# Cross-attention with LayerNorm: another order of the odd slot's work on TensorE, ScalarE and VectorE

## The chip, the core and the metric

The kernel runs on one core of a Trainium2 chip. A core has a matrix engine (TensorE, PE in the profile; its weight loads are PEld), a vector engine (VectorE, DVE), an engine for activation functions (ScalarE, ACT), a general engine (GpSimd, POOL) and SyncE (SP), which here only issues transfers. Each engine works through its own queue in order; semaphores make an instruction wait for one on another engine. The metric is the device time of one execution, in microseconds (us).

## The reference

Four batches of 2048 rows of x (512 wide) attend, in 16 heads of 32, to 77 rows of a context; then output projection, residual and LayerNorm:

```python
qs = (q @ wq).reshape(Bq, Lq, H, HD).transpose(0, 2, 1, 3)
ks_ = (k @ wk)...;  vs = (v @ wv)...
scores = jnp.einsum('bhqd,bhkd->bhqk', qs, ks_) / jnp.sqrt(jnp.float32(HD))
scores = jnp.where(mask[:, None, :, :], -jnp.inf, scores)
attn_w = jax.nn.softmax(scores, axis=-1)
attn = jnp.einsum('bhqk,bhkd->bhqd', attn_w, vs)
out = attn.transpose(0, 2, 1, 3).reshape(Bq, Lq, H * HD) @ wo + q
mu = jnp.mean(out, axis=-1, keepdims=True)
var = jnp.mean((out - mu) ** 2, axis=-1, keepdims=True)
return (out - mu) / jnp.sqrt(var + EPS) * gamma + beta
```

q is x, k and v are the context. All is float32.

## The kernel before

The 8192 rows are 64 tiles of 128 rows. Two tiles are a block, four a group; 16 tiles are a batch. Keys and values of all batches are made once at the start and stay on the chip. Each float32 matmul of a projection is three matmuls: operands are split into a high and a low part (hi*hi, hi*lo, lo*hi), so a projection of a tile is 12 matmuls of 128x128 by 512.

The stages of a tile t, with their engine and line:

- `load_xT`, `cast_xT` (ScalarE, L149), `split_xT` (GpSimd, L153): the transposed input, split in two parts; `q_visit` (TensorE, L160) and `q_evac` (VectorE, L177): queries, a quarter of a group in each slot.
- `scores` (TensorE, L284): 64 small matmuls of 32 rows into four banks of PSUM.
- `maxima` (VectorE, L298): for each of 16 heads, masked scores and their row maximum, each followed by a read of the accumulator.
- `exps` (ScalarE, L312): for each head, the exponential in place, with the row sum.
- `recip` (VectorE, L323) and `normalise` (GpSimd, L328): the reciprocal of the sums and one multiplication for all heads.
- `transp` (VectorE, L352) and `regroup` (12 transfers a block, issued by SP, L364): the weights transposed and laid out for the next product.
- `av` (TensorE, L382): the values' product of a block, 32 matmuls of 96x32 by 256; `av_hi` (ScalarE, L413) and `av_lo` (VectorE, L417): its result split into AH and AL.
- `o_proj` (TensorE, L446), `residual` (VectorE, L455), `moments` (VectorE L460 and L465, then four small operations on GpSimd, L469 to L472, in the odd tile).
- `scale` (ScalarE, L478), `affine` (GpSimd, L482 gamma and L483 beta), `store` (SP, L486).

A loop runs over 27 even tiles u (n = u/2 is the block). One turn has an even slot for tile u and an odd slot for tile u + 1. The stages overlap over several blocks: while tile u has its scores taken, the values' product belongs to block n - 2, the output projections to tiles u - 6 and u - 5, the scales to u - 8 and u - 7. The last ten tiles follow an order written out by hand (`ORDER`), which the change does not touch.

The order of the calls in the program is the order of each engine's queue; there is no scheduler. Three further things set the order of the work. All results of TensorE go through eight PSUM banks that are handed out in a ring, so a new tile waits until the tile eight allocations earlier is read out. `pbuf` (scores, exponentials and weights of a tile) has three buffers. AH and AL have two each, one block per buffer.

Twice per batch VectorE also prepares the mask of the next batch in the even slot: `mask_bias` (L264, L265) in the turn of the batch's tile 12, `mask_nan` (L269 to L271) in that of tile 14; this happens in the first three batches.

The order in the even slot is, on ScalarE: `cast_xT`, 12 exponentials of u, two scales, the last 4 exponentials of u. In the odd slot it is, on TensorE: scores, values' product, output projection, queries; on ScalarE: 4 exponentials of u + 1, the two casts of AH, 12 exponentials; on VectorE: 12 maxima of u + 1, reciprocal of u, 4 maxima, first AL, residual, second AL, transposition of u, moments, reciprocal of u + 1.

Of the kernel before, what the change touches and what calls it, by code (L numbers as in the profile page):

```python
# [19 lines left out]
H = 16  # L20
# [47 lines left out]
def xattn_layernorm(  # L68
# [26 lines left out]
    def bank(name):  # L95
        return ps.tile([P, 512], F32, tag="mm", name=name)
# [37 lines left out]
    def keys_of(h):  # L134
        return slice(TAIL_K, NK2) if h % 2 == 0 else slice(0, NK)
# [6 lines left out]
    def load_xT(g, c):  # L142
        fx[g, c] = sb.tile([P, 2, GRP], F32, tag="xtf", name=f"xtf_{g}_{c}")
        nc.sync.dma_start(fx[g, c], xT[g, :, c : c + 2])
# [29 lines left out]
    def q_evac(g, m):  # L174
        pq = qp.pop((g, m))
        if g:
            nc.vector.tensor_copy(qd[g][:, m, :], pq)  # L177
        else:
            nc.vector.tensor_copy(qd[0][:, m : m + 2, BLK:], pq.rearrange("p (m r) -> p m r", m=2))
# [45 lines left out]
    def values_evac(b):  # L225
        pv = vd.pop(b)[:NK2].rearrange("p (q a d) -> p q a d", a=2, d=HD)
        for a in range(2):
            nc.vector.tensor_scalar(  # L228
                vsb[:, b].rearrange("p (q a d) -> p q a d", a=2, d=HD)[:, :, a], pv[:, :, a], vm[:, a, 0:1], None, ALU.mult
            )  # L230
# [43 lines left out]
    def scores(t):  # L274
        qs = qd[t // 4]
        nmax[t] = sb.tile([P, H], F32, tag="nm", bufs=3, name=f"nm_{t}")
        sums[t] = sb.tile([P, H], F32, tag="sum", bufs=3, name=f"sum_{t}")
        sc = scs[t] = [bank(f"sc_{t}_{j}") for j in range(GH)]
        for g in range(NG):
            for half in range(0, P, P // 2):  # L280
                for j in range(GH):
                    q = slice(HD * j, HD * (j + 1))
                    r0 = (t % 4) * P + half
                    nc.tensor.matmul(  # L284
                        sc[j][half : half + P // 2, g * NK : (g + 1) * NK],
                        qs[q, g, r0 : r0 + P // 2],
                        kct[q, g, t // TPB, keys_of(j)],
                        start=True,
                        stop=True,
                    )  # L290

    def maxima(t, lo, hi):
        pb = pbuf[t % NPB]
        mb = bat[t // TPB][0]
        nm = nmax[t]
        for h in HEADS[lo:hi]:
            g, j = divmod(h, GH)
            nc.vector.tensor_tensor_reduce(  # L298
                pb[:, h // 2, (h % 2) * NK : (h % 2 + 1) * NK],
                scs[t][j][:, g * NK : (g + 1) * NK],  # L300
                mb[:, t % TPB, keys_of(h)],
                -1.0,
                3.0e38,
                ALU.add,
                ALU.min,
                accum_out=nm[:, h : h + 1],
            )

    def exps(t, lo, hi):
        pb = pbuf[t % NPB]  # L310
        for h in HEADS[lo:hi]:
            nc.scalar.activation(  # L312
                pb[:, h // 2, (h % 2) * NK : (h % 2 + 1) * NK],
                pb[:, h // 2, (h % 2) * NK : (h % 2 + 1) * NK],
                AF.Exp,
                bias=nmax[t][:, h : h + 1],
                scale=-1.0,
                accum_out=sums[t][:, h : h + 1],
            )

    def recip(t):
        ris[t] = sb.tile([P, H], F32, tag="ri", bufs=3, name=f"ri_{t}")
        nc.vector.reciprocal(ris[t], sums[t])  # L323

    def normalise(t):
        pv = pbuf[t % NPB][:, :, : 2 * NK].rearrange("p q (a k) -> p q a k", a=2)
        rv = ris[t].rearrange("p (q a) -> p q a", a=2)[:, :, :, None]
        nc.gpsimd.tensor_tensor(pv, pv, rv.to_broadcast((P, NP, 2, NK)), ALU.mult)  # L328
# [15 lines left out]
    def transp(t):  # L344
        b, tt = divmod(t, 2)
        if b not in bts:
            bts[b] = sb.tile([P, 5, 2 * NP * 32], F32, tag="B", name=f"B_{b}")
        if b < NBLK - 1:
            bt = bts[b].rearrange("p c (q t r) -> p c q t r", q=NP, t=2)[:, :, :, tt, :]
        else:  # L350
            bt = bts[b].rearrange("p c (t q r) -> p c q t r", q=NP, t=2)[:, :, :, tt, :]
        nc.vector.transpose(  # L352
            bt.rearrange("p c q r -> p q c r"),
            pbuf[t % NPB].rearrange("p q (c r) -> p q c r", c=5),
        )
# [81 lines left out]
    def o_proj(t):  # L437
        b, tt = divmod(t, 2)
        rs = slice(tt * P, tt * P + P)
        ah, al = at[b]  # L440
        first = t not in pos
        if first:
            pos[t] = bank(f"po_{t}")
        for c in range(NC_D):
            for n, (a, w) in enumerate(((ah, woh), (ah, wol), (al, woh))):
                nc.tensor.matmul(  # L446
                    pos[t],
                    a[:, c, rs],
                    w[:, c, :],
                    start=(first and c == 0 and n == 0),  # L450
                    stop=(c == NC_D - 1 and n == 2),
                )

    def residual(t):
        nc.vector.tensor_tensor(od[t], pos.pop(t), od[t], ALU.add)  # L455
# [124 lines left out]
    def pieces(u):  # L580
        return casts.get(u) or [((u + 8) // 4, u % 4)] * (u + 8 < 4 * NGRP)

    evac = [(0, 0)]
    for u in range(0, 2 * CUT, 2):
        n = u // 2
        m, k = divmod(u, TPB)

        for q in pieces(u + 2):
            if u >= 4:
                load_xT(*q)  # L590
        for t in (u - 4, u - 3):
            if t >= 0:
                load_x(t)
        scores(u)
        maxima(u, 0, H // 2)
        for q in evac:
            q_evac(*q)
        maxima(u, H // 2, H)
        for q in pieces(u):
            cast_xT(*q)  # L600
        exps(u, 0, 3 * H // 4)
        for v in list(vd):
            values_evac(v)
        for q in pieces(u):
            split_xT(*q)
        if u == 0:
            mask_bias(0, slice(1, TPB))
            split_wv()
        if u >= 6:
            o_proj(u - 6)  # L610
        for v in {2: (0,), 4: (2, 3)}.get(u, ()):
            values(v)
        for q in visits(u):
            q_visit(*q)
        if u >= 6:
            residual(u - 6)
            moments(u - 6)
        if u == 4:
            transp(2)
        if u:  # L620
            transp(u - 1)
            regroup(n - 1)
        if u >= 8:
            scale(u - 8)
            scale(u - 7)
        exps(u, 3 * H // 4, H)
        if u >= 8:
            affine(u - 8)
        for q in visits(u):
            q_evac(*q)  # L630
        if u == 0:
            load_wo()
            nc.gpsimd.memset(ident, 0.0)
            nc.gpsimd.affine_select(ident, ident, [[-1, P]], ALU.not_equal, 1.0, base=0, channel_multiplier=1)
        if u == 2:
            split_wo(0)
            split_wo(1)
        if k == TPB - 6 and m + 1 < NB:
            load_mask(m + 1)
        if k == TPB - 4 and m + 1 < NB:  # L640
            mask_bias(m + 1)
        if k == TPB - 2 and m + 1 < NB:
            mask_nan(m + 1)

        scores(u + 1)
        maxima(u + 1, 0, 3 * H // 4)
        recip(u)
        maxima(u + 1, 3 * H // 4, H)
        exps(u + 1, 0, H // 4)
        normalise(u)  # L650
        if u >= 8:
            affine(u - 7)
        for v in list(vd):
            values_evac(v)
        if u >= 4:
            av(n - 2)
            av_hi(n - 2, 0)
            av_hi(n - 2, 1)
        exps(u + 1, H // 4, H)
        if u >= 5:  # L660
            o_proj(u - 5)
        if u >= 4:
            av_lo(n - 2, 0)
        if u >= 5:
            residual(u - 5)
        if u >= 4:
            av_lo(n - 2, 1)
        if u != 2:
            transp(u)
        for v in {2: (1,)}.get(u, ()):  # L670
            values(v)
        evac = visits(u + 1)
        for q in evac:
            q_visit(*q)
        if u == 2:
            load_xT(*pieces(4)[0])
        if u >= 5:
            moments(u - 5)
        if u == 0:
            mask_nan(0)  # L680
        if u == 2:
            split_wo(2)
            split_wo(3)
        recip(u + 1)
        normalise(u + 1)
        if u >= 8:
            store(u - 8)
            store(u - 7)
# [87 lines left out]
```

## Time and profile before

| what | value |
|---|---|
| median of 3 runs | 534.55 us (533.18 to 534.91) |
| the profiled execution | 533.62 us |
| its span, first to last instruction | 531.8 us |
| granted TensorE clock, mean | 0.996 |
| TensorE busy | 514.6 us, 97% |
| VectorE busy | 485.3 us, 91% |
| ScalarE busy | 459.4 us, 86% |
| GpSimd busy | 401.1 us, 75% |

The span falls into a start (to about 81 us, where tile 8 begins), 23 even turns of the loop (to 431 us) and the tail. A row of the timeline gives start, duration, engine, line, operation, the tiles written and read with their shapes, and in brackets how long the engine stood idle before and what released it. Matmuls overlap in the rows, so what a group of them takes is read from its start to the start of the next group. The chain of waits is followed back from the last instruction, so it names at each moment what the end depended on.

### The profile page before, as it was taken

The numbers are of one execution on the slowest core, as the hardware profiler recorded it, in microseconds if no ns is written. First come the engines' busy times: TensorE is split into PE (matmuls) and PEld (weight loads), VectorE is DVE, ScalarE is ACT, GpSimd is POOL, SyncE is SP. The second block draws the span as 40 slices with busy tenths as digits, with TensorE's granted clock in tenths as the row PEclk, the third lists the DMA queues.
The fourth block names the chain that finished last, engine by engine and source line by source line (L and its number), as shares of the span: only waits on it lengthen the run. The fifth ranks groups of instructions, "written<-read, shape, count | busy, mean of one in ns | idle before, by whom it ended". The sixth has DMA issues, their size and how long they took to land.

```text
span 531.8 us, 20432 instructions
## 1 busy us (share of the span) xinstructions
PE 514.6 (97%) x6858; PEld 393.0 (74%) x6858; DVE 485.3 (91%) x2592; ACT 459.4 (86%) x2215; POOL 401.1 (75%) x363
## 2 busy tenths in 40 slices
PE   8999999999999999999999999999999999998994
PEld 6977677777777777777777777777777777775672
DVE  5689889999999899889998998889999989999897
ACT  5687799998899999998899999998899999998500
POOL 0626537998799988887899888888799988665751
PEclk9999999999999999999999999999999999999998
DMA  8934757888778788887778788779777865859844
GB/s 303 403 119 110 216 148 183 234 210 221 212 185 219 216 226 211 217 208 206 200 201 226 206 222 220 190 188 254 188 201 215 229 187 160 220 141 272 230 135 158
DMA packets 58712, 110.24 MB, mean 207 GB/s; under 512 B 9392, under 2 KB 11056, under 8 KB 58608
## 3 DMA queue, kind: packets, MB, share of 16 engines
q1 hardware_dynamic: 55424, 102.64, 70.2%
q0 software_dynamic: 2304, 5.24, 3.5%
q10 hardware_dynamic: 880, 1.05, 0.8%
q8 instruction: 55, 0.90, 0.7%
q14 instruction: 49, 0.40, 0.2%
HBM read 41.79 MB, written 16.78 MB: 110 GB/s over the span
## 4 chain that ended last, share of the span: by engine, by line
PE 29%; ACT 28%; DVE 26%; DMA 9%; issue 3%; SPq 3%; POOL 1%; DVEq 0%; ACTq 0%
ACT pbuf L312 23%; PE po L446 10%; PE pq L160 9%; DVE pbuf L298 7%; DVE B L352 5%; DMA PT<-B 4%; PE pa L382 3%; PE sc L284 3%; DVE q L177 3%; DMA o<-x 3%; ACT AH L413 3%; SPq L364 2%; DVE st L460 2%; ACT o L478 2%; PE pk L186 1%
## 5 line engine op out<-in xcount | busy, mean ns | idle before, releaser
L312 ACT ACTIVATE pbuf<-pbuf,nm 128x77 f32<-128x77 f32 x1024 | 353.2, 356 | 30.0 <-DVE nm L298 24.8
L312 ACT ACTIVATION_READ_ACCUMULATOR pbuf<-pbuf,nm 128x1 f32 x1024 | 201.4, 197 | 0.0
L328 POOL TENSOR_TENSOR pbuf<-pbuf,ri 128x1232 f32<-128x1232 f32 x63 | 142.9, 2270 | 58.2 <-DVE ri L323 44.5
L298 DVE CUSTOM_DVE_ANT_0 pbuf<-sc,mb 128x77 f32<-128x77 f32 x1024 | 168.8, 230 | 3.1 <-PE sc L284 3.1
L446 PE MATMUL po<-woh,AH 128*128 128x512 f32 x256 | 108.6, 424 | 0.0
L446 PE MATMUL po<-wol,AH 128*128 128x512 f32 x256 | 100.2, 391 | 0.0
L446 PE MATMUL po<-woh,AL 128*128 128x512 f32 x256 | 100.1, 391 | 0.0
L160 PE MATMUL pq<-xth,wqh 128*128 128x512 f32 (+1 forms) x256 | 98.5, 385 | 0.1
L160 PE MATMUL pq<-xtl,wqh 128*128 128x512 f32 (+1 forms) x256 | 97.9, 382 | 0.0
L160 PE MATMUL pq<-xth,wql 128*128 128x512 f32 (+1 forms) x256 | 97.9, 382 | 0.0
L352 DVE STREAM_TRANSPOSE B<-pbuf 128x1280 f32<-128x1280 f32 x64 | 95.5, 1493 | 2.5 <-POOL pbuf L328 1.8
L298 DVE DVE_READ_ACCUMULATOR2_ANT nm<- 128x1 f32 x1024 | 84.3, 82 | 0.0
L284 PEld LDWEIGHTS sc<-kct,q 32*64 32x64 f32 x4096 | 51.9, 130 | 23.6 <-issue 16.5
L153 POOL TENSOR_TENSOR xtl<-xtf,xth 128x1024 fp32r<-128x1024 f32 x28 | 67.1, 2398 | 2.8 <-ACT xth L149 2.8
L382 PE MATMUL pa<-PT,vsb 96*32 96x256 f32 x992 | 60.2, 381 | 7.5 <-DMA o<-x 1.9
L483 POOL TENSOR_TENSOR o<-o,bet 128x512 f32<-128x512 f32 x48 | 63.2, 1316 | 3.8
L446 PEld LDWEIGHTS po<-woh,AH 128*128 128x128 f32 x256 | 48.0, 187 | 23.2 <-DVE nm L298 6.2
L284 PE MATMUL sc<-kct,q 32*64 32x77 f32 x4096 | 62.5, 238 | 0.4 <-DVE vsb L228 0.4
L482 POOL TENSOR_TENSOR o<-o,gam 128x512 f32<-128x512 f32 x48 | 61.8, 1287 | 0.6 <-ACT o L478 0.3
L446 PEld LDWEIGHTS po<-woh,AL 128*128 128x128 f32 x256 | 48.1, 188 | 10.9 <-DVE AL L417 0.3
L160 PEld LDWEIGHTS pq<-xth,wqh 128*128 128x128 f32 x256 | 48.1, 188 | 10.5 <-PE pq L160 0.5
L446 PEld LDWEIGHTS po<-wol,AH 128*128 128x128 f32 x256 | 48.2, 188 | 9.5 <-issue 1.4
(106 smaller groups left out, 670.9 us busy)
## 6 DMA issues: line engine op xcount, KB each, us to landing
PT<-B SPq DMA_DIRECT2D x346, 128.0 KB
xtf<-xT SPq DMA_DIRECT2D x28, 512.0 KB
o<-x SPq DMA_DIRECT2D x56, 256.0 KB
out<-o SPq DMA_DIRECT2D x56, 256.0 KB
PT<-B POOLq DMA_DIRECT2D x21, 128.0 KB, 5.1
o_end<-x SPq DMA_DIRECT2D x8, 256.0 KB
out<-o_end SPq DMA_DIRECT2D x8, 256.0 KB
xtf<-xT SPq DMA_DIRECT2D x4, 256.0 KB
```

The costliest lines, as they stand in the source:

```text
L153: nc.gpsimd.tensor_tensor(l, fx.pop((g, c)), h.bitcast(F32), ALU.subtract)
L160: nc.tensor.matmul(pq, w[:, c, m * P : (m + 1) * P], r[:, c, rs], start=(n == 0), stop=(n == 11))
L177: nc.vector.tensor_copy(qd[g][:, m, :], pq)
L284: nc.tensor.matmul(sc[j][half : half + P // 2, g * NK : (g + 1) * NK], qs[q, g, r0 : r0 + P // 2], kct[q, g, t // TPB, keys_of(j)], start= ...
L298: nc.vector.tensor_tensor_reduce(pb[:, h // 2, (h % 2) * NK : (h % 2 + 1) * NK], scs[t][j][:, g * NK : (g + 1) * NK], mb[:, t % TPB, keys_ ...
L312: nc.scalar.activation(pb[:, h // 2, (h % 2) * NK : (h % 2 + 1) * NK], pb[:, h // 2, (h % 2) * NK : (h % 2 + 1) * NK], AF.Exp, bias=nmax[t ...
L328: nc.gpsimd.tensor_tensor(pv, pv, rv.to_broadcast((P, NP, 2, NK)), ALU.mult)
L352: nc.vector.transpose(bt.rearrange("p c q r -> p q c r"), pbuf[t % NPB].rearrange("p q (c r) -> p q c r", c=5),)
L382: nc.tensor.matmul(pas[b, g // 2][HD * j : HD * (j + 1), (g % 2) * BLK : (g % 2 + 1) * BLK], vsb[:, 2 * b // TPB, HD * h : HD * (h + 1)], ...
L446: nc.tensor.matmul(pos[t], a[:, c, rs], w[:, c, :], start=(first and c == 0 and n == 0), stop=(c == NC_D - 1 and n == 2),)
L482: nc.gpsimd.tensor_tensor(o, o, gam, ALU.mult)
L483: nc.gpsimd.tensor_tensor(o, o, bet, ALU.add)
```

## The change

In the even slot all 16 exponentials of u run ahead of the two scales. In the odd slot the reciprocal of u stands ahead of all 16 maxima of u + 1; 12 exponentials of u + 1 run before the casts of AH and 4 after them; the output projection and its residual come before the values' product; and the transposition of u comes before both AL on VectorE. GpSimd's and SP's queues keep their order, and no instruction is added or removed.

```diff
@@ even slot
         for q in pieces(u):
             cast_xT(*q)
-        exps(u, 0, 3 * H // 4)
+        exps(u, 0, H)
...
             scale(u - 8)
             scale(u - 7)
-        exps(u, 3 * H // 4, H)
         if u >= 8:
             affine(u - 8)
@@ odd slot
+        recip(u)
         scores(u + 1)
-        maxima(u + 1, 0, 3 * H // 4)
-        recip(u)
-        maxima(u + 1, 3 * H // 4, H)
-        exps(u + 1, 0, H // 4)
+        maxima(u + 1, 0, H)
         normalise(u)
+        exps(u + 1, 0, 3 * H // 4)
         if u >= 8:
             affine(u - 7)
         for v in list(vd):
             values_evac(v)
+        if u >= 5:
+            o_proj(u - 5)
+            residual(u - 5)
         if u >= 4:
             av(n - 2)
             av_hi(n - 2, 0)
             av_hi(n - 2, 1)
-        exps(u + 1, H // 4, H)
-        if u >= 5:
-            o_proj(u - 5)
+        exps(u + 1, 3 * H // 4, H)
+        if u != 2:
+            transp(u)
         if u >= 4:
             av_lo(n - 2, 0)
-        if u >= 5:
-            residual(u - 5)
-        if u >= 4:
             av_lo(n - 2, 1)
-        if u != 2:
-            transp(u)
```

## The prediction

> **What bounds the kernel now.** I read the page first, then one pair of tiles by the windows, then the chain of waits, then the timeline of each engine. In the page, TensorE is busy nearly all the time:
>
> ```profile
> PE 514.6 (97%) x6858; PEld 393.0 (74%) x6858; DVE 485.3 (91%) x2592; ACT 459.4 (86%) x2215; POOL 401.1 (75%) x363
> ```
>
> One pair of tiles of the steady part, from the start of its even scores to the next, as a window (length, then busy time of TensorE, its weight loads, VectorE, ScalarE, GpSimd; granted clock):
>
> ```profile
> 217.93:233.11 15.18, 15.00 (x209) 11.57 (x208) 13.43 (x79) 14.45 (x70) 13.19 (x11) 1.00 0.80 214
> ```
>
> TensorE has 0.18 us to spare in 15.18, ScalarE 0.73, VectorE and GpSimd near 2, at granted clock 1.00. The chain of waits in the same stretch runs on TensorE alone (start, duration, group):
>
> ```profile
> 218.00 0.88 PE sc L284 x52
> 218.88 2.92 PE po L446 x12
> 221.80 2.72 PE pq L160 x12
> 224.52 0.97 PE sc L284 x52
> 225.50 0.09 issue
> 225.59 1.93 PE pa L382 x32
> 227.52 2.94 PE po L446 x12
> 230.46 2.72 PE pq L160 x12
> ```
>
> The even slot (first three rows) takes 6.52 us, the odd one 8.66. ScalarE is the next bound. Its one stop per pair is ahead of the even tile's exponentials, for the maxima:
>
> ```profile
> 219.21 0.36 ACT L312 ACTIVATE pbuf<-pbuf,nm 128x77 f32<-128x77 f32 x1 [0.73 <-DVE nm L298]
> ```
>
> So ScalarE, when late, can win back about 0.8 us a pair. The question is whether that survives.
>
> **TensorE.** No instruction is added or removed; the order on GpSimd's and SP's queues is unchanged. In the odd slot the order becomes scores, output projection, values' product, queries. The tail of the kernel shows these neighbours already:
>
> ```profile
> 436.08 2.92 PE pq L160 x12
> 439.00 1.86 PE pa L382 x32
> 440.87 0.88 PE sc L284 x52
> 441.75 2.94 PE pq L160 x12
> ```
>
> A full-width group between scores and values' product takes 2.92, one between two tiled groups 2.94, the values' product 1.86, scores 0.88. The new odd slot is 0.88 + 2.92 + 1.86 + 2.94 = 8.60, a gain of 0.06 a pair; over the 23 pairs from tile 8 to tile 54, 1.4 us, if TensorE stays the bound. Bounds: 8.40 if the switch from projection to values' product cost nothing (2.72 in place of 2.92), 8.69 if the 0.09 of issue came back.
>
> The Trainium skill, page "TensorEngine Tiling (Array Packing)", Key Properties, says that changing the tiling mode drains TensorE. The change makes one more passage between full and tiled matmuls per pair; by that rule, with about 0.1 us per drain as an estimate from the 0.09 above, it would cost some 2 us over the pairs. The rows of the tail say that the dear switch is the present one, between two tiled forms (0.97 + 0.09 against 0.88), so the trace does not bear the loss out; neither decides the sum.
>
> **VectorE: a new ring of waits.** Three moves lengthen one path. The two scales of finished tiles (L478) stand behind 16 exponentials instead of 12; GpSimd's affine of the tile (L482, L483) waits for the first of them and stands ahead of normalise(u); and on VectorE transp(u), which waits for normalise(u), now stands ahead of both av_lo, of the moments, of recip(u+1), and so of the next even tile's maxima. These feed the next exponentials. That closes a ring, one turn per pair. Its pieces:
>
> ```profile
> 32.95 2.26 POOL L328 TENSOR_TENSOR pbuf<-pbuf,ri 128x1232 f32<-128x1232 f32 x1 [6.29 <-DVE ri L323]
> ...
> 215.32 0.69 DVE L455 TENSOR_TENSOR o<-po,o 128x512 f32<-128x512 f32 x1 [1.59 <-PE po L446]
> 215.93 0.68 DVE L417 TENSOR_TENSOR AL<-pa,AH 128x512 fp32r<-128x512 f32 x1
> 216.53 1.50 DVE L352 STREAM_TRANSPOSE B<-pbuf 128x1280 f32<-128x1280 f32 x1
> 217.95 0.65 DVE L460 BATCH_NORM_STATS2 st<-o 128x6 f32<-128x512 f32 x1
> 218.64 0.18 DVE L465 BATCH_NORM_AGGREGATE mv<-st 128x2 f32<-128x6 f32 x1
> 218.74 0.22 DVE L323 RECIPROCAL ri<-sum 128x16 f32<-128x16 f32 x1
> 218.87 0.24 DVE L298 CUSTOM_DVE_ANT_0 pbuf<-sc,mb 128x77 f32<-128x77 f32 x1
> ...
> 262.00 4.12 ACT pbuf L312 x24
> 285.37 0.82 ACT L478 ACTIVATE o<-o,rn 128x512 f32<-128x512 f32 x1
> 286.27 1.28 POOL L482 TENSOR_TENSOR o<-o,gam 128x512 f32<-128x512 f32 x1 [0.15 <-ACT o L478]
> 287.63 1.29 POOL L483 TENSOR_TENSOR o<-o,bet 128x512 f32<-128x512 f32 x1
> ```
>
> From the first exponential: 16 exponentials 5.50 (4.12 for 12 of them with their accumulator reads); scale to gam 0.90 (285.37 to 286.27, a row that waited); gam to bet 1.36; bet 1.29; normalise 2.26; transposition 1.42 (216.53 to 217.95); two av_lo at 0.60 (215.93 to 216.53); stats 0.69; aggregate 0.10; reciprocal 0.13; first maximum to first exponential 0.34 (218.87 to 219.21). Sum: 15.19. In the kernel before the same ring has 12 exponentials and no av_lo: 1.38 and 1.20 less, 12.6, which ScalarE's own 14.4 hides.
>
> So the ring equals TensorE's new 15.1 within its error. I bound it by 14.9 (if GpSimd, like VectorE in these rows, where 216.53 + 1.50 lies past 217.95, starts an operation some 0.08 before the last has ended, three times) and 15.5 (0.08, as between the scale's end and gam, at four more hand-offs). Taken: 15.19, the sum of the rows. Steadily it costs nothing; but lateness of ScalarE, which the kernel before wins back, is now never won back.
>
> **Where ScalarE becomes late.** Six pairs carry mask work for the next batch on VectorE, between the even tile's query copy and the odd tile's maxima: three times L264 and L265, three times L269 to L271.
>
> ```profile
> 240.78 1.30 DVE L264 TENSOR_SCALAR mb<-m 128x1232 bf16<-128x1232 uint8 x1
> 242.00 1.40 DVE L265 TENSOR_SCALAR mb<-m 128x304 bf16<-128x304 uint8 x1
> 243.65 0.36 ACT L312 ACTIVATE pbuf<-pbuf,nm 128x77 f32<-128x77 f32 x1 [2.17 <-DVE nm L298]
> 257.00 1.42 DVE L269 TENSOR_REDUCE nz<-m 128x16 f32<-128x1232 uint8 x1
> ...
> 259.24 0.23 DVE L298 CUSTOM_DVE_ANT_0 pbuf<-sc,mb 128x77 f32<-128x77 f32 x1
> ```
>
> The third row: ScalarE stood 2.17 us for the odd tile's maxima. The reciprocal, now ahead of them, adds 0.25: it waits for the sixteenth exponential, here long done, so nothing but its own time. Of 2.42, 0.73 is taken up by the stop quoted above: 1.7 late. The other mask pair has 2.24 of work (257.00 to 259.24) where the first has 2.54: 1.4 late. Three of each: 9.3 us, all of it kept.
>
> How much of it TensorE can ignore: the next output projection needs the first av_lo. In the new ring that ends 14.7 after the even scores begin (1.28 to the first exponential, 12.73 of the ring's pieces to the end of the transposition, 0.69); the third matmul of the next projection wants it at 15.1 + 0.88 + 0.5 (two matmuls of 2.92/12) = 16.5. That is 1.8 to spare, so TensorE follows ScalarE once the latter is 1.8 late, that is from the first mask pairs (tile 16) on.
>
> **The start.** Tiles below 8 have no scales to separate the exponentials of two tiles, so the reciprocal ahead of the maxima now stops ScalarE:
>
> ```profile
> 63.61 0.25 DVE L323 RECIPROCAL ri<-sum 128x16 f32<-128x16 f32 x1 [1.48 <-ACT pbuf L312]
> 64.86 1.05 ACT L413 CAST AH<-pa 128x512 fp32r<-128x512 f32 x2
> 66.11 0.50 PE L446 MATMUL po<-woh,AH 128*128 128x512 f32 x1
> 84.56 0.38 ACT L312 ACTIVATE pbuf<-pbuf,nm 128x77 f32<-128x77 f32 x1
> 432.61 0.36 ACT L312 ACTIVATE pbuf<-pbuf,nm 128x77 f32<-128x77 f32 x1 [0.61 <-DVE nm L298]
> ```
>
> Before, ScalarE went straight on while VectorE waited 1.48. After, it waits for reciprocal and first maximum: 0.6 in tiles 4 and 6 each, of which a later stop takes part; tile 8 starts 0.9 late. The cast AH (64.86) stands eight exponentials further back, 2.75 + 0.6 later, so the first output projection (66.11) comes about 3 later. TensorE loses there the lead it had; afterwards ScalarE decides.
>
> **What else moves, at no cost.** residual(u-5) ahead of the transposition: its projection ends earlier, so VectorE's wait of 1.6 us goes, and the wait for normalise(u) comes late in its place (in the ring). The casts AH behind 12 exponentials instead of 4: the values' product itself is 2.9 later, and ScalarE reaches them after it. The affines end later and with them two stores on SP; behind these stand loads whose data are wanted a pair later. The regrouping transfers follow transp(u-1), which does not move, and are wanted a pair later.
>
> **The sum.** ScalarE reaches tile 8 at 84.56 + 0.9 = 85.5 and tile 54 at 85.5 + 23 x 15.19 + 9.3 = 444.2. Before: 432.61. That is 11.6 late; TensorE, with its 1.8 to spare, is 9.8 late. I let the tail keep 9.8: the profiled 533.62 (span 531.8 and 1.8 around it) becomes 543.4. The runs' median is 0.93 above the profiled execution, so 544.
>
> **Rivals.**
> 1. *The lateness is won back.* If the ring is 14.8 or less, 0.3 a pair comes back; six pairs lie between mask pairs, and only 3.1 - 1.8 = 1.3 of each double reaches TensorE: 3 x 1.3 + 3 at the start - 1.4 gives +5.5, 540; without the start's share 537. For it: the overlaps of 0.08. Against: eleven pieces read from rows would have to be 0.4 too long together.
> 2. *Faster.* TensorE stays the bound and its odd slot falls to 8.40, the bound above: 0.26 x 23 = 6.0 won, less 3 of the start, 531.5. It decides only if the ring stays under 14.9; the rows of 2.92 and 2.94 speak against.
> 3. *A longer ring,* 15.5, hand-offs paid in full: 23 x 0.3 more, 551.
> 4. *Nothing happens:* gain and loss meet, 534.5; only the late start being hidden would allow it.
>
> **How the numbers follow.** Forecast (540 to 548) 0.55; rival 1 (537 to 540) 0.20; rival 3 0.10; rival 4 0.05; rival 2 0.10. A measurement of this kernel tells about 0.3%, 1.6 us. Slower: 0.85. The range 536.5 to 549 leaves out rivals 2 and 4 and the outer part of 3. With cases of one sign holding 0.85, no second range is needed.
>
> **What would show it.** Right: GpSimd's gam waits for the scale (ACT o L478) in nearly every pair; VectorE waits for normalise at its transposition; TensorE stops in the even output projection for AL in the mask pairs; pairs of 15.2 and six of 16.5 to 16.9; ScalarE's tile 8 at 85.5. Wrong: pairs below 15.0, ScalarE still stopping 0.7 for the maxima in each pair, or mask pairs followed by pairs of 14.4 on ScalarE.

## The result, and the profile after

| | before | after |
|---|---|---|
| median | 534.36 us | 539.64 us (538.21 to 540.22) |
| profiled execution | 533.62 us | 538.21 us |
| span of it | 531.8 us | 536.4 us |
| scores of tile 8 begin | 80.83 us | 82.90 us |
| scores of tile 54 begin | 431.33 us | 433.94 us |
| exponentials of tile 8 begin | 84.56 us | 84.26 us |
| exponentials of tile 54 begin | 432.61 us | 436.86 us |

The ratio is 1.0098, with a 95% interval of 1.0071 to 1.0124: the changed kernel is 1.0% slower, 5.3 us. The forecast was 544, 9.5 slower.

The page of the changed kernel: TensorE's busy time is up, for the same 6858 matmuls, ScalarE's unchanged, and two groups that hardly waited before now wait, VectorE's transposition for normalise (2.5 us before, 29.9 after) and GpSimd's gam for the scale (0.6 before, 14.8 after; the number behind the bar is idle time ahead of the group). The two groups before:

```profile
L352 DVE STREAM_TRANSPOSE B<-pbuf 128x1280 f32<-128x1280 f32 x64 | 95.5, 1493 | 2.5 <-POOL pbuf L328 1.8
...
L482 POOL TENSOR_TENSOR o<-o,gam 128x512 f32<-128x512 f32 x48 | 61.8, 1287 | 0.6 <-ACT o L478 0.3
```

The changed kernel:

```profile
PE 520.7 (97%) x6858; PEld 387.7 (72%) x6858; DVE 479.4 (89%) x2592; ACT 460.0 (86%) x2215; POOL 401.3 (75%) x363
...
DVE 38%; ACT 22%; POOL 14%; PE 10%; DMA 8%; SPq 4%; issue 3%; DVEq 0%; ACTq 0%; POOLq 0%
...
L352 DVE STREAM_TRANSPOSE B<-pbuf 128x1280 f32<-128x1280 f32 x64 | 95.6, 1495 | 29.9 <-POOL pbuf L328 27.9
...
L482 POOL TENSOR_TENSOR o<-o,gam 128x512 f32<-128x512 f32 x48 | 63.8, 1328 | 14.8 <-ACT o L478 14.8
```

The chain of waits of the changed kernel (start, duration, group) no longer follows TensorE. It goes round the ring:

```profile
206.96 3.60 ACT pbuf L312 x21
210.56 0.10 issue
210.66 1.90 ACT pbuf L312 x11
212.56 0.71 ACT o L478
213.27 0.07 issue
213.34 1.29 POOL o L482
...
214.72 1.28 POOL o L483
215.99 2.22 POOL pbuf L328
218.22 0.02 issue
218.24 1.51 DVE B L352
219.75 1.17 DVE AL L417 x2
220.92 0.61 DVE st L460
221.53 0.02 issue
221.56 0.18 DVE mv L465
221.74 0.14 DVE ri L323
221.88 0.09 DVE pbuf L298
...
222.07 1.05 ACT pbuf L312 x5
```

One turn is 222.07 - 206.96 = 15.11 us. TensorE's plain pairs are a little shorter than before: from tile 20 to tile 28 they average 15.14, against 15.20. The windows of a plain pair and of a pair that carries mask work, in the changed kernel:

```profile
189.18:204.35 15.17, 15.17 (x209) 11.32 (x209) 13.41 (x79) 14.44 (x70) 13.22 (x12) 1.00 0.83 215
249.80:265.28 15.48, 15.48 (x209) 11.24 (x208) 15.01 (x82) 14.22 (x69) 13.06 (x12) 1.00 0.76 201
```

In the second, TensorE stands for AL. In its timeline the third matmul of the output projection, the first that reads AL, begins 0.39 after the one ahead of it; in the plain pair that step is 0.23 (190.41 to 190.64). The step behind it is longer too, 0.34 in place of 0.23:

```profile
250.72 0.50 PE L446 MATMUL po<-woh,AH 128*128 128x512 f32 x1
251.05 0.40 PE L446 MATMUL po<-wol,AH 128*128 128x512 f32 x1
251.44 0.50 PE L446 MATMUL po<-woh,AL 128*128 128x512 f32 x1
251.78 0.40 PE L446 MATMUL po<-woh,AH 128*128 128x512 f32 x1
```

The starts of the even tiles' exponentials on ScalarE, one pair to the next, tell the rest. Before: 14.28 in pairs in which ScalarE is late, 15.2 in pairs in which it has caught up with TensorE, 15.9 to 16.6 in the mask pairs. After: 15.10 to 15.15 in every plain pair from tile 18 on, and 16.18 and 15.66 in each double of mask pairs. So the lateness of a mask pair stays. Against TensorE it falls from 2.5 to 1.2 between the second double and the third (tiles 32 to 44), but not because ScalarE wins it back: TensorE has stood, and its pairs there are the longer ones, 15.21 and more.

### The profile page after: what moved, and what is told of

Same layout as the page of the kernel before. It is cut to its first block, busy times and chain, and to the rows that moved or that the text cites. A ratio compares the mean times of both kernels' runs of the same rounds, so it can differ in the third digit from the quotient of the medians.

```text
span 536.4 us, 20477 instructions
## 1 busy us (share of the span) xinstructions
PE 520.7 (97%) x6858; PEld 387.7 (72%) x6858; DVE 479.4 (89%) x2592; ACT 460.0 (86%) x2215; POOL 401.3 (75%) x363
## 4 chain that ended last, share of the span: by engine, by line
DVE 38%; ACT 22%; POOL 14%; PE 10%; DMA 8%; SPq 4%; issue 3%; DVEq 0%; ACTq 0%; POOLq 0%
ACT pbuf L312 19%; DVE B L352 9%; POOL pbuf L328 7%; DVE pbuf L298 6%; DVE AL L417 6%; PE pq L160 5%; DMA PT<-B 4%; DVE st L460 4%; POOL o L483 4%; PE po L446 3%; POOL o L482 3%; SPq L364 3%; DVE q L177 2%; ACT o L478 2%; DMA stage_b<-wo 1%
## 5 line engine op out<-in xcount | busy, mean ns | idle before, releaser
L312 ACT ACTIVATION_READ_ACCUMULATOR pbuf<-pbuf,nm 128x1 f32 x1024 | 194.6, 190 | 0.0
L298 DVE CUSTOM_DVE_ANT_0 pbuf<-sc,mb 128x77 f32<-128x77 f32 x1024 | 166.3, 230 | 3.5 <-PE sc L284 3.5
L352 DVE STREAM_TRANSPOSE B<-pbuf 128x1280 f32<-128x1280 f32 x64 | 95.6, 1495 | 29.9 <-POOL pbuf L328 27.9
L160 PE MATMUL pq<-xth,wqh 128*128 128x512 f32 (+1 forms) x256 | 101.8, 398 | 2.7 <-DVE nm L298 2.7
L482 POOL TENSOR_TENSOR o<-o,gam 128x512 f32<-128x512 f32 x48 | 63.8, 1328 | 14.8 <-ACT o L478 14.8
L483 POOL TENSOR_TENSOR o<-o,bet 128x512 f32<-128x512 f32 x48 | 61.8, 1287 | 3.8
L446 PEld LDWEIGHTS po<-woh,AH 128*128 128x128 f32 x256 | 48.1, 188 | 15.5 <-issue 1.9
L160 PEld LDWEIGHTS pq<-xth,wql 128*128 128x128 f32 x256 | 48.5, 189 | 9.7
```

Of the source, the lines that this page charges most:

```text
L160: nc.tensor.matmul(pq, w[:, c, m * P : (m + 1) * P], r[:, c, rs], start=(n == 0), stop=(n == 11))
L298: nc.vector.tensor_tensor_reduce(pb[:, h // 2, (h % 2) * NK : (h % 2 + 1) * NK], scs[t][j][:, g * NK : (g + 1) * NK], mb[:, t % TPB, keys_ ...
L312: nc.scalar.activation(pb[:, h // 2, (h % 2) * NK : (h % 2 + 1) * NK], pb[:, h // 2, (h % 2) * NK : (h % 2 + 1) * NK], AF.Exp, bias=nmax[t ...
L352: nc.vector.transpose(bt.rearrange("p c q r -> p q c r"), pbuf[t % NPB].rearrange("p q (c r) -> p q c r", c=5),)
L446: nc.tensor.matmul(pos[t], a[:, c, rs], w[:, c, :], start=(first and c == 0 and n == 0), stop=(c == NC_D - 1 and n == 2),)
L482: nc.gpsimd.tensor_tensor(o, o, gam, ALU.mult)
```

## The experiments

Theory R (ring): ScalarE's lateness, made in the mask pairs, is kept, because the new ring is as long as TensorE's pair. Rival T: the order on TensorE costs by itself. In the table, the lateness of ScalarE is its first even exponential less TensorE's even scores, less the 1.28 us of a pair without lateness; the pairs are those of ScalarE. The kernel before, run beside each set, had medians of 533.8 to 534.4.

| kernel | median, us | ratio to before (95%) | plain pair when late | mask pairs | lateness at tile 54 |
|---|---|---|---|---|---|
| before | 534.3 | 1 | 14.28 | 16.57, 15.93 | 0.0 |
| changed | 539.64 | 1.0098 (1.0071 to 1.0124) | 15.11 | 16.18, 15.66 | 1.6 |
| scales after 12 | 537.65 | 1.0077 (1.0055 to 1.0098) | 14.88 | 16.60, 16.20 | 1.1 |
| affine behind normalise | 534.91 | 1.0017 (1.0001 to 1.0034) | 14.65 | 15.10, 15.90 | 0.0 |
| transposition behind AL | 556.85 | 1.0431 (1.0406 to 1.0455) | 15.46 | 17.33, 18.17 | 2.8 |
| reciprocal inside the maxima | 548.13 | 1.0265 (1.0236 to 1.0294) | 15.12 | 16.69, 17.52 | 0.1 |
| before, no mask work | 534.56 | 1.0004 (0.9987 to 1.0021) | 14.28 | none | 0.0 |
| changed, no mask work | 534.38 | 1.0000 (0.9985 to 1.0016) | never late | none | 0.0 |
| before with 16 in a run | 534.46 | 0.9996 (0.9983 to 1.0008) | 14.28 | 16.06, 15.54 | 0.0 |
| old start, affine behind | 531.00 | 0.9938 (0.9922 to 0.9953) | 14.42 | 15.12, 15.91 | 0.1 |

**The mask work left out, before and after.** The edit, the same in both kernels:

```diff
-            load_mask(m + 1)
-        if k == TPB - 4 and m + 1 < NB:
-            mask_bias(m + 1)
-        if k == TPB - 2 and m + 1 < NB:
-            mask_nan(m + 1)
+            bat[m + 1] = bat[0]
```

> The kernel before with the mask work of batches 1 to 3 left out (load, bias and row flags; all batches use batch 0's mask, so the output is another). Ring theory: the kernel before wins the lateness of its mask pairs back and TensorE loses only a few tenths there, so it gains 0 to 1 us: 533.6 us (532.8 to 534.5). Rival: the mask pairs cost every version the same on TensorE: some 4 us less, 530.

> The changed kernel with the same mask work left out (same other output). Ring theory: without lateness ScalarE reaches tile 54 at 84.3 + 23 x 15.11 = 431.8 and TensorE, the bound again, at about the same; the tail is as long as before (100.5): 534 to 536 us, 4 us less than the changed kernel, and 1 to 2 more than the kernel before without mask work (TensorE's start is 2 us later). Rival, the new order costs in every pair: 538 to 539, still 1% above the kernel before without mask work.

Measured: 534.56 and 534.38. The kernel before gains nothing, the changed one 5.3 us, and the two are equal. (Batches 1 to 3 then use the mask of batch 0, so both compute something else.) TensorE's new order, its later start and the ring cost nothing net as long as nothing makes ScalarE late: the whole loss passes through the mask pairs. This rules out rival T.

**The scales after 12 exponentials again.**

```diff
-        exps(u, 0, H)
+        exps(u, 0, 3 * H // 4)
...
             scale(u - 7)
+        exps(u, 3 * H // 4, H)
```

> The changed kernel with one part undone: the two scales again stand behind 12 of the even tile's 16 exponentials. Ring theory: GpSimd's affine starts 1.4 us earlier, the ring of waits falls from the 15.11 us seen after to about 13.7, ScalarE can win lateness back (its own loop with the wait for the reciprocal is about 14.9), so the 2.5 us by which it lags after the mask pairs are gone by the next batch and TensorE is the bound at 15.15 to 15.2 a pair: 535 us (534 to 536.5). Rival, TensorE's new order is what costs: no change against the changed kernel, 539 to 540.

Measured 537.65: 2.0 less than the changed kernel, though the two intervals overlap, and short of the forecast. In the profiled executions ScalarE reaches tile 54 at 435.00 instead of 436.86. The late pairs are 14.88 on ScalarE, as expected, so 0.3 is won back in each, but the mask pairs are 16.60 and 16.20, together 3.0 over 14.88 where the changed kernel has 1.6 over 15.11. Six plain pairs win back 2.0 of it: TensorE still stood 0.7 after the second double, and ScalarE enters the tail 1.1 late. A turn that wins back 0.3 is not enough here.

**The affine behind normalise.** Only GpSimd's queue changes:

```diff
-        if u >= 8:
-            affine(u - 8)
...
         normalise(u)
         exps(u + 1, 0, 3 * H // 4)
         if u >= 8:
+            affine(u - 8)
             affine(u - 7)
```

> The changed kernel with one move on GpSimd's queue: affine(u-8) stands behind normalise(u) instead of ahead of it, so that the scales and the affine are no part of the ring. Ring theory: the ring falls by some 3 us to below ScalarE's own 14.3 to 14.5; lateness is won back by 0.6 us a pair; no wait of VectorE for normalise at the odd slot's transposition; 534.5 us (533 to 536). Rival (TensorE's order): 539 to 540.

Measured 534.91. The lateness is gone (0.7 after a double of mask pairs, 0.1 a pair later, the pair between at 14.47 to 14.65), and with it all of the loss but 0.2% of the time. GpSimd's queue is the same length; only the scales and the affine no longer stand between the exponentials and normalise. The edit does a second thing, so it alone is no clean proof of the ring: mask work runs here while GpSimd is idle, and in the first mask pair takes half as long (last section). What that cannot explain is that the 0.7 that is left is won back within one pair, which the changed kernel never does.

**The transposition behind both AL again.**

```diff
-        if u != 2:
-            transp(u)
         if u >= 4:
             av_lo(n - 2, 0)
             av_lo(n - 2, 1)
+        if u != 2:
+            transp(u)
```

> The changed kernel with one part undone: the transposition of u stands behind both av_lo again, while the casts of AH stay behind 12 exponentials. Ring theory: another ring closes, through ScalarE: 16 exponentials 5.55, two scales 1.4, 0.2, 12 exponentials 4.2, two casts 1.0, second av_lo 0.6, transposition 1.4, stats, aggregate, reciprocal 0.95, 0.35 to the next exponential: 15.5 to 15.7 a pair; with 0.4 to 0.5 more in each of 23 pairs 547 us (544 to 551). Rival (TensorE's order): as the changed kernel, 539 to 540.

Measured 556.85, in the profile 554.9 of span. The plain pair is 15.46, just under the forecast range, and VectorE waits for the casts AH in 26 places. Waits of this kernel (waiting engine and line, what it waited for: us in total, times, longest):

```profile
DVE AL L417 <- ACT AH L413: 48.9, 26, 2.0
```

What the forecast left out is that the mask pairs grow: 17.33 and 18.17, 4.6 a double over 15.46 where the changed kernel has 1.6 over 15.11, three doubles. So the change's parts hang together: with the casts moved behind 12 exponentials, the transposition must not wait behind AL.

**The reciprocal inside the maxima again.**

```diff
-        recip(u)
         scores(u + 1)
-        maxima(u + 1, 0, H)
+        maxima(u + 1, 0, 3 * H // 4)
+        recip(u)
+        maxima(u + 1, 3 * H // 4, H)
```

> The changed kernel with one part undone: the reciprocal of u again stands behind 12 maxima of u+1. Ring theory: in plain pairs nothing (the affine ends later than the reciprocal either way, ring 15.1); in the six mask pairs normalise starts 0.9 later and the ring is some 0.6 longer, 3.6 in all, less about 1 for tiles 4 and 6, where ScalarE no longer waits for the reciprocal: 542 us (540.5 to 543.5). Rival: the reciprocal's place has no part in it, 539 to 540.

Measured 548.13. The plain pair is untouched, 15.12, as expected; the mask pairs cost 1.6 and 2.4 over it, 12.0 in three doubles, where 0.6 more than the changed kernel was forecast for each. Two things were missed. The longest mask pair has 2.95 us of mask work instead of 1.8, because one instruction was held up by GpSimd (last section). And lateness comes to 4 us after the second mask pair, so TensorE stands for AH and AL in one projection:

```profile
145.99 0.50 PE L446 MATMUL po<-woh,AH 128*128 128x512 f32 x1 [1.07 <-ACT AH L413]
147.56 0.50 PE L446 MATMUL po<-woh,AL 128*128 128x512 f32 x1 [0.85 <-DVE AL L417]
```

The stop adds nothing to the end by itself: ScalarE's 23 turns of 15.12 and the 12.0 already make up its way from tile 8 to tile 54 (84.80 to 444.61). The reciprocal ahead of the maxima is therefore a part that the new order cannot do without.

**Sixteen exponentials in a run, alone, on the kernel before.**

```diff
-        exps(u, 0, 3 * H // 4)
+        exps(u, 0, H)
...
             scale(u - 7)
-        exps(u, 3 * H // 4, H)
```

> The kernel before with one part of the change alone: 16 exponentials in a run ahead of the two scales. Ring theory: its ring grows by 1.4 us to some 14, still below ScalarE's 14.3 and TensorE's 15.2, so nothing: 534 us (533 to 535.3). Rival, the run of 16 costs by itself (scales, affines and stores later): 536 or more.

Measured 534.46, ratio 0.9996: nothing. The same edit that costs in the changed order is free in the old one, where late pairs on ScalarE stay at 14.28.

**The old order at the start, with the affine behind normalise.** On top of that kernel, the odd slots of tiles 4 and 6 keep the order of the kernel before:

```diff
+        if u in (4, 6):
+            scores(u + 1)
+            maxima(u + 1, 0, 3 * H // 4)
+            recip(u)
+            maxima(u + 1, 3 * H // 4, H)
+            exps(u + 1, 0, H // 4)
+            normalise(u)
...
+            av(n - 2)
+            av_hi(n - 2, 0)
+            av_hi(n - 2, 1)
+            exps(u + 1, H // 4, H)
...
+        else:
```

> The kernel with affine(u-8) behind normalise(u), and the odd slots of tiles 4 and 6 in the order of the kernel before. Its theory: with the ring short, what is left above the kernel before is TensorE's later start (82.3 against 80.8 at tile 8); that goes, and 0.04 to 0.06 us a pair for TensorE's new neighbours stays: 532.5 us, ratio 0.996 to 0.999. Rival: TensorE's gain a pair isn't real, ratio 1.000 to 1.002.

Measured 531.00, ratio 0.9938 (0.9922 to 0.9953): faster than both kernels, and than forecast. A plain pair in the windows:

```profile
200.80:215.93 15.13, 15.13 (x209) 11.30 (x209) 13.71 (x79) 14.48 (x70) 13.22 (x12) 1.00 0.80 207
```

From tile 8 to tile 54 TensorE takes 428.50 - 79.47 = 349.03, against 350.50 before: 1.5 us for the new neighbours, 0.064 a pair. The start is 1.4 shorter than before (79.47 against 80.83), which the forecast did not count: in the new order of tiles 0 and 2 the exponentials of tile 4 begin at 56.66 instead of 58.00.

## Why the prediction was right, and where its sizes were off

**TensorE's pair.** Right: 0.06 was forecast, 0.064 measured where TensorE is the bound. The rows of the tail priced the new neighbours rightly: in the last kernel above the odd slot takes 8.61 to 8.65, where 8.60 was forecast. The count of passages was off, without effect on the sum: per pair the new order has two more between full and tiled matmuls and one less between two tiled forms, while the prediction spoke of one more between full and tiled.

**The ring.** Right in kind and nearly in size: 15.11 measured, 15.19 taken, the bounds 14.9 and 15.5. In the timeline no piece is off by more than 0.06. The two largest: normalise starts 0.04 before bet has ended, as the lower bound supposed (1.24 from bet's start, 1.29 taken), and the first exponential comes 0.28 after the first maximum's start (221.79 to 222.07, 0.34 taken). bet starts 0.08 after gam's end, which the sum already had. The prediction named the waits that appeared, gam for the scale and the transposition for normalise. Over 23 pairs the 0.08 is 1.8 us too much.

**Where ScalarE becomes late.** The step that was mis-sized most: 1.7 and 1.4 a double, 9.3 in all; measured 1.07 and 0.55 over 15.11, 4.9 in all. ScalarE's stops ahead of the odd tile's exponentials, in the two mask pairs of the second double:

```profile
245.97 0.36 ACT L312 ACTIVATE pbuf<-pbuf,nm 128x77 f32<-128x77 f32 x1 [1.77 <-DVE nm L298]
...
261.64 0.36 ACT L312 ACTIVATE pbuf<-pbuf,nm 128x77 f32<-128x77 f32 x1 [1.26 <-DVE nm L298]
```

The step put them at 2.42 and 2.1. Of each, 0.73 is taken up by the stop ahead of the even tile, as it supposed: 1.77 and 1.26 less 0.73 leave 1.04 and 0.53. So the slack was right and the stops were taken too long. Most of that is the mask work, 2.54 and 2.24 us in the rows of before; after, counted in the same way to the start of the next operation, it is 2.03 (243.51 to 245.54) and 1.74 (259.46 to 261.20). The rows of before held waits for GpSimd, some of which the new order moves onto GpSimd (last section). In the second pair ScalarE also begins the even tile 0.51 after VectorE's first maximum (252.86 to 253.37), where the plain turn has 0.28, and that hides 0.2 more.

**The start.** Wrong in sign for ScalarE: tile 8 at 84.26, not 85.5, because tile 4 begins 1.35 earlier (56.65 against 58.00), which the step did not look at. With the reciprocal inside the maxima it begins at 57.55, so most of this is the earlier reciprocal in tiles 0 and 2; the rest was not pursued. For TensorE 3 was forecast and 2.07 came, but not by the late cast AH. In the turn of tile 4 TensorE stands for a PSUM bank, because the maxima that free it now come behind the reciprocal:

```profile
63.24 0.47 PE L160 MATMUL pq<-xth,wqh 128*128 128x512 f32 x1 [2.71 <-DVE nm L298]
```

From 64.7 to 68.1 its granted clock is then 0.50, which the mean of 0.993 hides. The kernel with the scales after 12 has the same queues up to tile 8; it stands 2.06 there, its clock does not fall, and its tile 8 begins at 81.97. So part of the 2.07 goes with the fall: 0.9 between these two executions, the longer stop included. With the reciprocal inside the maxima the stop at the queries is gone, and TensorE stands 2.03 for AH instead, at 67.76. None of this lasts: without mask work the changed kernel has such a stop too (2.65) and such a fall (62.7 to 66.1), and loses nothing.

**Spare of TensorE, and the tail.** The spare was given as 1.8, and TensorE's pairs bear it out: they lengthen, to 15.35 to 15.69, where ScalarE is 1.9 to 2.5 late, and stay at 15.13 to 15.23 where it is 1.7 late or less. The first double left only 1.4, so TensorE follows from tile 30 on, not from tile 16. At tile 54 ScalarE was 1.6 late. Letting the tail keep TensorE's lateness was wrong: TensorE was 2.6 late at tile 54, ScalarE 4.25, and the span ended 4.6 late. The tail follows ScalarE. Kept from ScalarE's 11.6 instead, the forecast would have been 1.8 higher, so this error hid part of the one in the mask pairs.

**The sum.** ScalarE at tile 54 was forecast for 444.2 and came at 436.86. Of the 7.3 between, 4.4 are the mask pairs, 1.8 the ring, 1.2 the start.

**The signs.** Of those named for being right, the waits of gam and of the transposition came, and TensorE's stop for AL; the mask pairs of 16.5 to 16.9 and tile 8 at 85.5 did not. One named for being wrong came as well: from tile 18 on ScalarE still stops 0.71 to 0.75 ahead of every even tile but the two behind mask work.

```profile
222.07 0.36 ACT L312 ACTIVATE pbuf<-pbuf,nm 128x77 f32<-128x77 f32 x1 [0.72 <-POOL rn L469]
```

It does not speak against the ring. The stop and ScalarE's own 14.4 make up the 15.11: it is what the ring leaves over, and ScalarE cannot use it. In the kernel before, the stop is nil in late pairs, which are 14.28. The sign was badly chosen.

**The rivals.** That the ring and the mask pairs decide is no luck; that the forecast is off by only 4.4 is so in part, as the tail's error took 1.8 off a sum that was too high. The time fell where rival 1 put it (540), but not for its reason: nothing to speak of was won back (late pairs of 15.11 against TensorE's 15.13 to 15.22); there was less to win back. A time like rival 2's (531.5) came only with the affine moved out of the ring and the old order at the start (531.00), and not for its reason: the odd slot never fell to 8.40.

## What to carry to other kernels

An engine that is not the bound may still need its slack: here ScalarE's 0.9 us a pair paid back the irregular pairs, and an order that closes a ring as long as the bound's period looks free in every plain pair and keeps each stall for good. When operations are moved, add up the ring that leads from one turn's operation back to the same one in the next, over all queues, and look for the irregular turns that rely on it being short. And the member of the ring whose result nothing in the turn needs (here the affine) is the one to move.

## What the runs showed of the hardware

I had not expected how VectorE and GpSimd exclude each other. Three of the mask's five instructions (L264, L265, L270) depend on what GpSimd does at the moment; L269 does not, and L271 never began well inside a GpSimd operation. With GpSimd idle, in the kernel with the affine behind normalise (timeline, VectorE):

```profile
241.74 0.78 DVE L264 TENSOR_SCALAR mb<-m 128x1232 bf16<-128x1232 uint8 x1
242.44 0.32 DVE L265 TENSOR_SCALAR mb<-m 128x304 bf16<-128x304 uint8 x1
256.84 1.41 DVE L269 TENSOR_REDUCE nz<-m 128x16 f32<-128x1232 uint8 x1
258.29 0.17 DVE L270 TENSOR_SCALAR nz<-nz 128x16 f32<-128x16 f32 x1
```

In the changed kernel L264 begins 0.06 ahead of GpSimd's gam and keeps its 0.78; gam is stretched from 1.28 to 1.87, and L265, now beside it, from 0.32 to 1.40:

```profile
243.51 0.78 DVE L264 TENSOR_SCALAR mb<-m 128x1232 bf16<-128x1232 uint8 x1
243.57 1.87 POOL L482 TENSOR_TENSOR o<-o,gam 128x512 f32<-128x512 f32 x1 [0.55 <-ACT o L478]
244.21 1.40 DVE L265 TENSOR_SCALAR mb<-m 128x304 bf16<-128x304 uint8 x1
```

In the kernel with the reciprocal inside the maxima bet begins 0.02 ahead of L270, which needs 0.17 alone: it takes 1.29 and ends 0.03 after bet.

```profile
139.48 1.28 POOL L483 TENSOR_TENSOR o<-o,bet 128x512 f32<-128x512 f32 x1
139.50 1.29 DVE L270 TENSOR_SCALAR nz<-nz 128x16 f32<-128x16 f32 x1
```

In the kernel before, L270 takes 0.64 to 0.67 in its three places and ends 0.03 after bet each time. L269, the reduction, takes 1.41 to 1.42 whatever GpSimd does. The Trainium skill, page "SBUF — State Buffer", section "Who interferes with whom", describes a pair of ports that VectorE, in some of its forms, and GpSimd hold exclusively for a whole instruction, so that the later one blocks; the rows agree with that, down to the order that decides who waits. In length they fall a little short of it: gam, kept out until L264 ends at 244.29 and then as long as alone, would end at 245.57 and ends at 245.44. What share of the 5.3 us goes through this was not measured by itself; mask work of 1.0 (241.74 to 242.76) in place of 2.1 us (243.51 to 245.61) is what it makes in the first mask pair.
